# An experts' layer between two attention stages: norm, logits, routing and row sends as steps of the first layer's blocks, the fallback in pieces behind the last block

## The chip, the cores and the metric

The kernel runs on one core of a Trainium2 chip. The metric is device time in microseconds (us) of one execution. The engines are PE (TensorE: matrix products, transposes), DVE (VectorE), ACT (ScalarE), POOL (GpSimd) and SP (SyncE, which here only issues DMAs).

## What is computed

The input x has 16 sequences of 256 tokens with 128 features, all f32: 4096 tokens. Four residual steps follow each other.

```python
x = x + linear_attention(norm(x))     # 32 heads of 4, two decays, a norm at its end
x = x + experts(norm(x))              # 8 experts, two per token, at most 1280 tokens each
x = x + decay_attention(norm(x))
x = x + local_attention_and_ffn(norm(x))   # 2 layers
```

The second step is the one that the change is about:

```python
probs = softmax(x_flat @ Wr.T)
scores, experts = top_k(probs, 2);  scores = scores / scores.sum(-1)
cap = 1280                                    # int(1.25 * 4096 * 2 / 8)
y_fb = ffn(x_flat, fw1, fb1, fw2, fb2)        # the fallback, for every token
y = 0; fallback = False
for e in range(8):
    match = (experts == e)
    elig = match.any(-1) & ~fallback          # tokens, in order
    pos = cumsum(elig) - 1
    kept, overflow = elig & (pos < cap), elig & (pos >= cap)
    y[kept] += ffn(x_flat[kept], W1[e], b1[e], W2[e], b2[e]) * weight
    y = where(overflow, y_fb, y); fallback = fallback | overflow
```

`ffn` is a gelu between two products (128 to 512 and back). A token that overflows an expert takes the fallback's output and takes part in no later expert.

## The kernel before

**Tiles and blocks.** The tokens form 32 tiles of 128 rows (NT), and 8 blocks of four tiles (NB). All of x stays in SBUF. "Normal" tiles hold tokens in the partitions; turned ones (`hT`) hold features in them.

**First stage, lines 263 to 563, by hand.** A class `Linear` (line 364) has the steps of one block as methods: `measure_x`, `rows_x`, `turn` (norm and transposes of the input), `rotate`, `raised`, `feature` (queries and keys), `gates`, `clip`, `spread_beta`, `value`, `weigh`, `scan` (446, a DVE scan of 128x512 for each of 2 decays m and of 5 columns cc), `product` (451, POOL, scan by query), `den`, `share`, `query`, `add` (477, PE sums of the products into the bank `y`), `gather`, `project` (486, into the bank `z`), `measure_z`, `rows_z` (the norm at the end) and `close` (502, three POOL operations of 128x512 that add the block's result to x). A class `Spread` (335) keeps mean and variance for one iteration; one square root on ACT serves all of them. The loop at 511 runs t = -2 to 9 under `tc.manual_schedule()`: the order of instructions in the program is the order on each engine. In iteration t, block t is scanned, t+1 is projected, t+2 is measured and turned, t-1 is finished, and t-2 is closed.

**Second stage, lines 565 to 819, by a planner.** Outside the hand-written order a planner orders the instructions of each engine by their costs and due times. SP issues the loads of the last stage's weights (570 to 587). Then come the statistics of all 32 tiles (helper, lines 245 and 246), normalisation on DVE (655), transposes (656), the logits (660, 661), the routing of all 32 tiles at once (679 to 744), and the 64 sends (748 to 753): each is an indirect DMA issued by POOL that scatters the 128 rows of a tile from `hn` to the slots of their expert in `xs`, in DRAM. The routing counts, for each of the 8 experts in turn, the tokens ahead (two PE products with constant tables and a DVE scan over tiles, 718 to 733), since an overflow changes what later experts see. For each block, lines 773 to 792 add the experts' bias by weights (`w9`, turned by PE, times `b2row`, line 783) and the fallback's output by its weight (788). The fallback and the experts share `ffn` (663): four pairs of `ph` products with gelu on ACT (669) into `hid`, then `py` products. The experts (795 to 817) read `xs` in 8 x 3 chunks of 512, 512 and 256 rows (`xe`, SP, line 800), turn them (805), copy them (807, DVE), run `ffn`, and store `ye` into `ys` (811, 812).

**Last stage, from line 822.** Rows are fetched from `ys` by 64 gathers (1035, POOL), then decay attention, local attention and the last ffn follow. The change leaves it alone.

In the listing, `mm` (line 128) is the helper that records most products, so these groups have the line L128 in the profile.

Of the kernel before, what the change touches and what calls it, by code (L numbers as in the profile page):

```python
# [18 lines left out]
P = 128  # L19
BATCH = 16  # L20
SEQ = 256
D = 128
# [31 lines left out]
def _layout():  # L54
    at, n = {}, 0
    for name, width in (
        ("ident", P), ("sel", 4 * P), ("blk", NH0), ("rep4", P), ("cos", SEQ), ("sin", SEQ),
        ("behind", P), ("rep8", P), ("xpos", 4 * 2 * DH), ("desc", NE),
    ):
        at[name] = (n, width)  # L60
        n += width
# [3 lines left out]
def _tables():  # L65
# [39 lines left out]
    put("desc", np.tile(np.arange(NE, 0, -1, dtype=f4), (P, 1)))  # L105
    return c
# [16 lines left out]
def tile_kernel(ctx: ExitStack, tc: tile.TileContext, i: dict, out: bass.AP, last: int = 4):  # L123
# [124 lines left out]
    def rstd(mv, n=NT):  # L248
        r = small.tile([P, n], F32, tag="rstd", name="rstd")
        act.activation(r, mv[:, :, 1], AF.Sqrt, bias=eps)  # L250
        dve.reciprocal(r, r)
        return r

    def normalize(eng, o, a, mv, r, n):
        eng.tensor_scalar(o, a, mv[:, n, 0:1], r[:, n : n + 1], ALU.subtract, ALU.mult)

    def transposed(ps, name, n=P):
        t = ps.tile([P, BW], F32, tag="tr", name="wtr")
        pe.transpose(t[:, :n], nat[name], ident[:n, :n])
        return t[:, :n]  # L260


    with ExitStack() as c:
# [6 lines left out]
        po = c.enter_context(tc.tile_pool(name="a_po", bufs=1, space=PSUM))  # L270
# [64 lines left out]
        class Spread:  # L335


            def __init__(self):
                self.mv = wk.tile([P, 8, 2], F32, tag="mv", name="mv", bufs=3)
                self.lo, self.hi = 8, 0  # L340
# [5 lines left out]
            def sqrt(self):  # L346
                if self.lo > self.hi:
                    return
                self.rs = wk.tile([P, 8], F32, tag="rs", name="rs", bufs=3)
                self.nm = wk.tile([P, 8], F32, tag="nm", name="nm", bufs=3)  # L350
# [13 lines left out]
        class Linear:  # L364
# [6 lines left out]
            def measure_x(self, sp):  # L371
                for j in range(4):
                    sp.take(4 + j, x[:, 4 * self.b + j, :])

            def rows_x(self, sp):
                self.h = wtile("h", 2)
                for j in range(4):
                    sp.row(self.h[:, js(j)], x[:, 4 * self.b + j, :], 4 + j)
# [107 lines left out]
            def project(self):  # L486
                self.z = po.tile([P, BW], F32, tag="po", name="po")
# [5 lines left out]
            def measure_z(self, sp):  # L493
                for j in range(4):
                    sp.take(j, self.z[:, js(j)])

            def rows_z(self, sp):
                self.o = wk.tile([P, 4, D], F32, tag="o", name="o")
                for j in range(4):
                    sp.row(self.o[:, j, :], self.z[:, js(j)], j)  # L500
# [7 lines left out]

        blocks = [Linear(b) for b in range(NB)]
        with tc.manual_schedule():  # L510
            for t in range(-2, NB + 2):
# [4 lines left out]
                sp = Spread()  # L516
                do(0, "scan", 0, HD0)
                do(0, "scan", 1, HD0)
                do(0, "product", 0, HD0)
                do(0, "product", 1, HD0)  # L520
                do(2, "measure_x", sp)
                do(1, "rotate", "k")
                do(-1, "add", 1, HD0 - 1)
                do(-1, "gather")
                do(1, "rotate", "q")
                do(0, "den")
                do(-1, "project")
                do(1, "gates")
                do(0, "share")
# [770 lines left out]
```

## Time and profile before

| | us |
|---|---|
| median of 3 runs | 1548.76 (1547.97 to 1551.07) |
| the profiled execution | 1548.69 |
| its span, from first to last instruction | 1546.9 |
| PE busy | 1240.1 (80%) |
| DVE busy | 979.6 (63%) |
| POOL busy | 831.6 (54%) |
| ACT busy | 770.6 (50%) |
| granted clock of PE, mean | 0.900 |
| end of the last product of block 7 (first stage) | 253.3 |
| end of block 7's `close` | 266.0 |
| first and last send | 327.8 and 408.4 |
| first matmul of an expert's chunk (transposes, line 805) | 453.8 |
| start of the last stage (about) | 616.8 |

The busy times are shares of the whole span and so say little about a stage. The profile's page also has the span in 40 slices of 38.7 us, with a digit for each engine (9: 90% or more busy) and for PE's clock. A group of instructions is named by its line, engine, operation and tiles (out<-in), with its count, its busy time and the mean of one in ns. The chain of waits goes back from the last instruction to what released each; "issue" in it is time in which an engine waited for nothing that the profile shows, "remote" in a wait is a semaphore whose setter the profile doesn't name. SPq is SP's DMA queue, PEld is the load of PE's weights.

### The profile page before, as it was taken

What the parts mean: (1) busy time and instruction counts of PE and PEld (TensorE: products, weight loads), DVE (VectorE), ACT (ScalarE), POOL (GpSimd) and SP (SyncE); (2) the same over time, 40 slices, a digit from 0 to 9 for tenths busy, and PEclk for the clock granted to TensorE, in tenths of its full rate; (3) what the DMA queues carried; (4) which work ended last, traced back from release to release, by engine and by line L of the source; (5) the groups of instructions that cost most, each with busy time, mean ns of one, the idle gap of its engine ahead of it and who ended that gap; (6) DMA issues with size and microseconds to landing.
All of it is one profiled execution on the core that took longest, in us unless ns stands there. A gap on an engine that the chain in (4) does not pass through costs nothing.

```text
span 1546.9 us, 26264 instructions
## 1 busy us (share of the span) xinstructions
PE 1240.1 (80%) x9793; PEld 817.4 (53%) x9793; DVE 979.6 (63%) x2316; ACT 770.6 (50%) x1478; POOL 831.6 (54%) x822
## 2 busy tenths in 40 slices
PE   5788785870299999265688788899999999999996
PEld 2334433650267777132355465666666666666673
DVE  4999985540021111357887787888778887878862
ACT  4443521310033333134556657776777767677653
POOL 1577775047400000668877765776676767767521
PEclk9989896775599999567898899999999999999998
DMA  7300000201102221100111111111111111111110
GB/s 225 136 1 1 1 1 32 65 26 51 56 11 68 69 68 34 36 24 17 39 29 32 29 24 23 26 24 33 26 26 31 26 31 33 38 33 26 38 34 16
DMA packets 67450, 59.41 MB, mean 38 GB/s; under 512 B 16905, under 2 KB 53754, under 8 KB 67322
## 3 DMA queue, kind: packets, MB, share of 16 engines
q1 hardware_dynamic: 62402, 48.12, 11.7%
q0 software_dynamic: 4096, 8.40, 1.7%
q8 instruction: 78, 1.28, 0.3%
q10 hardware_dynamic: 824, 1.20, 0.2%
q14 instruction: 50, 0.41, 0.1%
HBM read 21.78 MB, written 16.78 MB: 25 GB/s over the span
## 4 chain that ended last, share of the span: by engine, by line
PE 41%; DVE 24%; issue 9%; ACT 7%; DMA 1%; POOL 0%; POOLq 0%; another core or an unknown queue 0%; ACTq 0%; DVEq 0%
PE pm L128 9%; PE py L128 7%; PE pq L128 7%; PE ph L128 7%; DVE rot L878 3%; PE S L128 3%; DVE ss L879 3%; ACT hn L1158 2%; DVE x L1044 2%; DVE bnst L245 2%; PE pm L996 2%; PE pm L974 2%; PE pm L932 1%; DVE o L991 1%; DVE ex L963 1%
## 5 line engine op out<-in xcount | busy, mean ns | idle before, releaser
L881 POOL TENSOR_TENSOR t<-t,tabs 128x512 f32<-128x512 f32 x128 | 164.4, 1285 | 141.0 <-ACT t L876 140.6
L669 ACT ACTIVATE hid<-ph,b1c 128x512 f32<-128x512 f32 (+1 forms) x128 | 79.8, 633 | 184.9 <-PE ph L128 119.6
L883 POOL TENSOR_TENSOR rot<-rot,t 128x512 f32<-128x512 f32 x128 | 163.1, 1274 | 10.0
L921 POOL TENSOR_TENSOR rot<-rot,rn 128x512 f32<-128x512 f32 x128 | 130.7, 1042 | 40.4 <-DVE rn L900 40.4
L878 DVE TENSOR_TENSOR rot<-pq,tabs 128x512 f32<-128x512 f32 x128 | 87.7, 685 | 79.1 <-ACT t L876 77.7
L128 PE MATMUL pq<-wqkv,hT 128*128 128x512 f32 x256 | 134.4, 651 | 0.8 <-DVE rot L878 0.8
L998 ACT COPY oT<-pm 128x512 f32<-128x512 f32 x64 | 37.1, 580 | 188.6 <-PE pm L996 183.3
L841 POOL MEMSET mhalf<- 128x1 f32 x1 | 0.1, 104 | 206.4 <-ACT hid L669 206.4
L453 POOL TENSOR_TENSOR s<-s,q 128x512 f32<-128x512 f32 x64 | 83.7, 1317 | 38.2 <-DVE s L449 20.2
L750 POOL DMA_INDIRECT xs<-hn,r_into x64 | 62.4, 975 | 76.9 <-DVE r_into L740 57.7
L962 DVE TENSOR_REDUCE ng<-S 128x4 f32<-128x512 f32 x128 | 87.4, 683 | 23.0 <-PE S L128 21.2
L811 DVE COPY ye<-py 128x512 f32<-128x512 f32 (+1 forms) x24 | 14.5, 603 | 135.5 <-PE py L128 135.5
L963 DVE TENSOR_TENSOR ex<-S,ng 128x512 f32<-128x512 f32 x128 | 88.5, 692 | 4.6
L874 ACT ACTIVATE sq<-pq 128x512 f32<-128x512 f32 x128 | 77.6, 606 | 27.0 <-PE pq L128 22.0
L879 DVE TENSOR_REDUCE ss<-sq 128x8 f32<-128x512 f32 x128 | 86.5, 676 | 0.0
L128 PEld LDWEIGHTS pm<-vs,pT 128*64 128x64 f32 x1024 | 64.5, 137 | 38.8 <-issue 11.1
L128 PEld LDWEIGHTS py<-w,hid 128*128 128x128 f32 x640 | 77.6, 192 | 12.9 <-issue 8.6
L996 PE MATMUL pm<-cf,o 128*128 128x128 f32 x256 | 43.3, 294 | 49.6 <-DVE o L991 49.6
L128 PE MATMUL ph<-xT,w 128*128 128x512 f32 (+1 forms) x192 | 75.3, 528 | 7.7 <-DVE xT L807 7.7
L128 PE MATMUL py<-w,hid 128*128 128x128 f32 x640 | 80.0, 277 | 0.0
L967 ACT ACTIVATE ex<-ex 128x512 f32<-128x512 f32 x128 | 76.4, 662 | 3.1 <-DVE ex L963 2.8
L932 PE MATMUL pm<-cf,rot 128*128 128x128 f32 x512 | 70.2, 276 | 9.3 <-POOL rot L921 6.5
(293 smaller groups left out, 3345.4 us busy)
## 6 DMA issues: line engine op xcount, KB each, us to landing
vs<-v SPq DMA_DIRECT2D x128, 130.0 KB
xs<-zeros SPq DMA_DIRECT2D x10, 512.0 KB
w<-in_L_ffn_W_dram SPq DMA_DIRECT2D x16, 256.0 KB
xe<-xs SPq DMA_DIRECT2D x16, 256.0 KB
ys<-ye SPq DMA_DIRECT2D x16, 256.0 KB
x<-in_L_attn_x_dram SPq DMA_DIRECT2D x8, 256.0 KB
out_dram<-x SPq DMA_DIRECT2D x8, 256.0 KB
up<-u SPq DMA_DIRECT2D x32, 56.0 KB
```

The lines of the kernel that those rows point to most:

```text
L128: pe.matmul(o, lhsT, rhs, start=start, stop=stop)
L453: pool.tensor_tensor(s, s, self.f["q"] if cc == HD0 else self.q[m], ALU.mult)
L669: act.activation(hid[:, ci, :width], t[:, :width], AF.Gelu, bias=b1c[:, bias0 + ci : bias0 + ci + 1])
L874: act.activation(sq, ps, AF.Square)
L878: dve.tensor_tensor(heads(rot[:, k, :]), heads(ps), wide(tabs[l][:, 2 * k, a, :]), ALU.mult)
L879: dve.tensor_reduce(ss[:, j, k, :], heads(sq), AX.X, ALU.add)
L881: pool.tensor_tensor(heads(t2), heads(t2), wide(tabs[l][:, 2 * k + 1, a, :]), ALU.mult)
L883: pool.tensor_tensor(halves(rot[:, k, :]), halves(rot[:, k, :]), halves(t2)[:, :, ::-1, :], ALU.add)
L921: pool.tensor_tensor(ro, ro, rn, ALU.mult)
L932: pe.transpose(ps[:, hp * P : (hp + 1) * P], self.rot[:, k, hp * P : (hp + 1) * P], ident)
L962: dve.tensor_reduce(ng[:, q, :], self.S[q], AX.X, ALU.max, negate=True)
L963: dve.tensor_tensor(ex[:, q], self.S[q], ng[:, q, :].unsqueeze(2).to_broadcast([P, 4, P]), ALU.add)
```

## The change

1. **Norm, logits.** After `close`, a block's x is measured (`measure_n`), and one iteration later normalised on ACT (`rows_n`, formerly DVE), turned (`turn_n`) and given its logits. All statistics share the iteration's `Spread` (12 columns, formerly 8). `close` moves from block t-2, ahead of the products, to block t-1, behind the first half of them. `add` is grouped: the four of m=0 at cc=0, the four of m=1 at the start of the next iteration. The bank of `z` is now that of `y`, and the bank that came free serves the routing.
2. **Routing by groups of tiles.** `Route(lo, hi).steps()` is a generator that handles a range of tiles, and hands back at each `yield`; `tick()` runs it to the next. Tiles 0 to 7 begin at t=4, 8 to 15 at t=6, 16 to 23 behind the loop, then 24 to 27 and 28 to 31. The first group can't overflow (1024 tokens, 1280 slots) and counts all experts at once; the others go expert by expert, and start from the counts of the group before.
3. **Sends.** `send(3)` behind `query` and `send(2)` at the end of an iteration put sends on POOL, each behind a memset of a 128x1 tile, `spare`; 20 of the 64 are issued inside the loop (t=4 to 7). Those of the tail follow as 6, 2, and then whatever is routed.
4. **Tail.** The loop ends at t=7. The rest of blocks 6 and 7 is written out by hand, with pieces of the fallback between (`fill`). There are 64 pieces: 32 of a `ph` product and gelu, 32 of eight `py` products. The fallback's result overwrites the turned tile in `hT`, and waits there.
5. **Second stage.** It keeps the shares, `w9`, and the experts; the bias and the fallback's weighted result are added by `residual(e)`, one block behind each expert.

The diff, cut to its core:

```diff
@@ class Linear
             def project(self):
-                self.z = po.tile([P, BW], F32, tag="po", name="po")
+                self.z = py.tile([P, BW], F32, tag="py", name="po")
...
+            def measure_n(self, sp):
+                for j in range(4):
+                    sp.take(8 + j, x[:, 4 * self.b + j, :])
+            def rows_n(self, sp):
+                for j in range(4):
+                    sp.row(hn[:, 4 * self.b + j, :], x[:, 4 * self.b + j, :], 8 + j)
+            def turn_n(self):
+                pt = bank("nt")
+                for j in range(4):
+                    pe.transpose(pt[:, js(j)], hn[:, 4 * self.b + j, :], ident)
+                act.copy(cols_n(self.b), pt)
+            def logits(self):
+                pl = bank("pl")
+                for j in range(4):
+                    mm(pl[:, j * NE : (j + 1) * NE], hT[:, 4 * self.b + j, :], wr)
+                dve.tensor_copy(lg[:, 4 * self.b : 4 * self.b + 4, :].rearrange("p n e -> p (n e)"), pl[:, : 4 * NE])
+        class Route:
+            def steps(self):
...
+                if hi * P <= CAP and lo == 0:
+                    m = match.rearrange("p e n -> p (e n)")
...
+                    mm(pos, con("behind"), m)
+                    mm(tot, ones, m)
+                    yield
...
+                else:
...
+                    for e in range(NE):
...
+                        dve.tensor_tensor(el, match[:, e, :], ok, ALU.mult)
+                        mm(tot, ones, el)
+                        mm(pos, con("behind"), el)
+                        yield
+                        before = Route.counts[:, e, -1:] if lo else 0.0
+                        dve.tensor_tensor_scan(run[:, e, :], ones[:, 0:n], tot, before, ALU.mult, ALU.add)
+                        dve.tensor_tensor(r, run[:, e, :], pos, ALU.add)
+                        dve.scalar_tensor_tensor(over, r, float(CAP), el, ALU.is_gt, ALU.mult)
+                        dve.tensor_tensor(ok, ok, over, ALU.subtract)
...
+                for j in range(lo, hi):
+                    rows.extend([(j, 0), (j, 1)])
+        def send(most):
+            for _ in range(min(most, len(rows))):
+                j, k = rows.pop(0)
+                pool.memset(spare, 0.0)
+                sent.append(pool.indirect_dma_start(
+                    out=xs, out_offset=bass.IndirectOffsetOnAxis(ap=into[k][:, j : j + 1], axis=0),
+                    in_=hn[:, j, :], in_offset=None, bounds_check=SLOTS - 1, oob_is_err=False,
+                ))
+        def fallback():
...
+            for b in range(NB + 1):
+                hid[b] = []
+                for ci in range(NIC):
+                    if b < NB:
+                        t = bank("fh")
+                        mm(t, fw1[:, ci * P : (ci + 1) * P], cols_n(b))
+                        h = wtile(f"kv{ci}")
+                        at_ = NE * NIC + ci
+                        act.activation(h, t, AF.Gelu, bias=b1c[:, at_ : at_ + 1])
+                        hid[b].append(h)
+                        yield
+                    if b:
+                        outward(b - 1, ci)
+                        yield
@@ the loop
-            for t in range(-2, NB + 2):
+            for t in range(-2, NB):
...
-                sp = Spread()
+                sp, later = later, Spread()
+                if t == 4:
+                    work.append(Route(0, 8).steps())
+                elif t == 6:
+                    work.append(Route(8, 16).steps())
                 do(0, "scan", 0, HD0)
                 do(0, "scan", 1, HD0)
+                tick()
                 do(0, "product", 0, HD0)
                 do(0, "product", 1, HD0)
                 do(2, "measure_x", sp)
+                tick()
                 do(1, "rotate", "k")
-                do(-1, "add", 1, HD0 - 1)
+                tick()
+                for cc in range(HD0):
+                    do(-1, "add", 1, cc)
                 do(-1, "gather")
...
-                do(-2, "close")
+                tick()
+                send(3)
                 sp.scales()
...
                 do(2, "rows_x", sp)
+                do(-2, "rows_n", sp)
                 for cc in range(HD0):
                     do(0, "product", 0, cc)
...
+                do(-1, "close")
                 do(1, "feature", "k")
...
                 for cc in range(HD0):
                     do(0, "scan", 1, cc)
+                    tick()
                     do(1, "weigh", cc)
-                    do(0, "add", 0, cc)
+                    if cc == 0:
+                        for c2 in range(HD0):
+                            do(0, "add", 0, c2)
...
                     if cc == 1:
                         do(1, "feature", "q")
                         do(2, "turn")
+                        do(-2, "turn_n")
+                        if t == 1:
+                            prepare()
+                    if cc == 2:
+                        do(-2, "logits")
                     do(0, "product", 1, cc)
-                    if cc:
-                        do(0, "add", 1, cc - 1)
+                do(-1, "measure_n", later)
                 do(1, "spread_beta", 1)
+                send(2)
@@ the tail
+            work.append(Route(16, 24).steps())
+            tick(2)
...
+            last_b.project()
+            both(2)
+            send(6)
+            last_b.measure_z(sp)
...
+            last_b.close()
+            send(2)
...
+            last_b.logits()
+            work.append(Route(24, 28).steps())
+            work.append(Route(28, 32).steps())
+            while work:
+                both(1)
+                send(NT)
+            for _ in fb:
+                pass
@@ the second stage
-        for b in range(NB):
+        def residual(b):
...
-            ffn(hT[:, 4 * b : 4 * b + 4, :].rearrange("p n t -> p (n t)"), BW, fw1, NE * NIC, fw2, add_fallback)
+            for n in range(4 * b, 4 * b + 4):
+                dve.scalar_tensor_tensor(x[:, n, :], hT[:, n, :], w9[:, n, NE : NE + 1], x[:, n, :], ALU.mult, ALU.add)
 
         for e in range(NE):
...
                 ffn(xT[:, :width], width, w1[:, e, :], e * NIC, w2[:, e, :, :], keep)
+            residual(e)
```

`both(n)` is n times a `tick()` and a piece of the fallback. The statistics, normalisation, logits, routing, sends and fallback of the second stage (lines 644 to 661, 679 to 753 and 773 to 792) are removed. `prepare` makes `wr` and `b1c` (formerly lines 597 to 603).

## The prediction

> **What bounds the kernel now.** I read four views: the 40 slices, then the windows (busy time by stage), then the chain and the waits where PE stands, then the timeline around its two ends. The slices first:
>
> ```profile
> PE   5788785870299999265688788899999999999996
> DVE  4999985540021111357887787888778887878862
> POOL 1577775047400000668877765776676767767521
> PEclk9989896775599999567898899999999999999998
> ```
>
> One slice is 38.7 us. The 2nd to the 7th are the first layer's loop, with DVE highest; the 8th to the 16th are the experts' stage, and in it the 10th holds a PE of 0 and the 11th of 2, while POOL stands at 7 and 4. From 616.8 us the last stage runs, 930.1 us, which the change doesn't touch. By stage (window, its length, busy PE, PEld, DVE, ACT, POOL, clock, DMA):
>
> ```profile
> 127.55:155.49 27.94, 23.15 (x128) 11.30 (x128) 25.82 (x43) 11.59 (x26) 20.23 (x19) 0.94 0.00 1
> 360.00:380.00 20.00, 0.00 (x0) 0.00 (x0) 0.00 (x0) 0.00 (x0) 15.43 (x16) 0.50 0.15 53
> 414.00:616.80 202.80, 194.98 (x1143) 148.63 (x1144) 35.60 (x72) 70.34 (x116) 1.01 (x3) 0.98 0.17 49
> ```
>
> The first is one iteration of the loop: DVE bounds it, with 2.1 us to spare. The third is the end of the fallback and the experts: PE bounds it, 96% busy. In the second only POOL works. What stands there, by the chain (start, us, what), by the waits between 336 and 432 (engine, line, what it waited for: us in all, times, longest) and by the costliest groups:
>
> ```profile
> 340.54 2.88 PE py L128 x24
> ...
> 352.37 61.72 issue
> 414.08 2.07 PE bw L128 x8
> ```
> ```profile
> ACT hid L669 <- remote: 63.9, 1, 63.9
> ...
> PE bw L128 <- issue: 61.7, 1, 61.7
> DVE x L788 <- remote: 54.6, 1, 54.6
> ```
> ```profile
> L750 POOL DMA_INDIRECT xs<-hn,r_into x64 | 62.4, 975 | 76.9 <-DVE r_into L740 57.7
> ```
>
> The 64 sends run from 327.8 to 409.4, one each 1.27 us (0.97 and 0.30 of issue). PE goes on for 16 us of them, some 12 sends; then it gives one matmul per 0.7 us, and from 352.4 nothing until 414.1, 4.7 us after the last send. The chain calls it "issue": no semaphore of another engine ended it. That the dense row of sends does it is my reading; its onset after 12 sends I use below. So between the last product of block 7 (ends 253.3) and the first expert (453.8) lie 200 us, of which 62 are PE standing, 61 are norm and routing with every engine half idle, and the rest is mostly fallback.
>
> **Part 1, the loop.** Each of its iterations gets statistics of x after `close` (4 x 0.40 = 1.6 us of DVE), a row step (4 x 0.4 ACT), 4 transposes (0.60 PE), a copy (0.58 ACT), logits (1.0 PE) and their copy (0.19 DVE). ACT has 16 us free in 27.94, and hides its part; PE has 4.8. What is not hidden is the order: turn, copy, turn_n, copy, logits, copy stand in front of `scan(1,3)` on DVE, 0.6+0.58+0.6+0.58+1.0+0.19 = 3.55, less some 1.4 that the copy and the product before it already covered: +2.1. The statistics at the end add 1.6 to DVE, of which about 0.6 lies beside PE's own chain: +1.0. So t=2..5: 4 x 3.1 = 12.4; t=6 without the statistics' wait: 2.1; `prepare` at t=1: 1.3. At t=7, `close` (3 x 1.27 on POOL) now stands ahead of the products of the second half, and no next block's work covers it, +4.1; and the two sends that t=6 issues at its end stand ahead of the first products (2 x 1.45, less 0.8 in which POOL waits for the scans), +2.1: 6.2. In t=5 and t=6 I leave that to the next part. The grouped adds cost nothing more: 8 such matmuls ran in 1.06 us, as long as 2 alone:
>
> ```profile
> 142.06 1.06 PE L128 MATMUL y<-s,cfa 128*32 128x512 f32 x8
> 143.41 1.04 PE L128 MATMUL y<-s,cfa 128*32 128x512 f32 x2 [0.28 <-POOL s L453]
> ```
>
> Routing on DVE: the operations of 128x32 in the old routing took 0.18 to 0.22 us, those of 128x256 0.42; for 8 tiles (64 columns) I take 0.21. Route(0,8) has 26: 5.5. Route(8,16) has 65: 13.6, less 2.6 that fall into DVE's gaps: 11. Bounds for the two: all hidden in gaps (2.1 us x 4 = 8.4 less), or each operation also waiting for PE's answer (8 answers at 0.9, as the old one did: +7). Sum for the loop: 12.4+2.1+1.3+6.2+5.5+11 = +38.5; block 7's last product ends at 292 (bounds 280 and 305).
>
> **Part 2, the sends in the loop.** 20 of them, 5 in each of t=4..7, each with a memset of 0.1 us: 1.45 us of POOL. POOL has 20.23 + 7.25 = 27.5 of an iteration that is now about 31: hidden, at nothing; if it isn't, up to 20 x 1.45 = 29 us. Behind a send on POOL stand the products, for which PE's adds wait. An indirect transfer beside a busy DVE is shown in the last stage: its gathers (line 1035) took 997 to 1092 ns, middle 1026, against 972 in the idle burst, so +5%.
>
> The Trainium skill ("SBUF — State Buffer", section "SBUF: two separate sides") speaks against this: a DMA issued by GpSimd needs the port that VectorE's fast modes hold, and one of some 620 ns took 3100 beside such work. By that, 20 sends would cost an estimated 20 x 2.5 = 50 us, and the forecast would come to 1565 instead. This case's gathers at 1026 ns beside a DVE 80% busy speak for the row.
>
> **Part 3, the tail.** POOL from 292: 8 sends 11.6, `close` 3.8, 2 sends 2.9: 310. Block 7's norm to logits ends near 320. Then Route(24,28) and Route(28,32), each 8 experts at about 1.9 us (2.16 with matmuls between, 1.86 alone in the old one) and 6 around them: 21, so 341 and 362. The sends follow in rows of 20, 8 and 8; the last 8 begin at 362 and end at 373.6, land by 376 (a send landed 2.3 us after its issue).
>
> The fallback: 32 pieces of 2 ph (1.02) and 32 of 8 py (0.83): 58 us of PE. 38 pieces lie beside norm and routing, 26 behind: 26 x 0.95 = 25, so 387. The weights of the last stage (SP: `fa` to `maskb`, lines 573 to 587), formerly issued from 266.06 to 278.8, wait for `spare`'s last memset (372) and take 12.7 us of SP; the experts' first rows stand behind them: 388, with their landing. That cover is the fallback; without it these are 12 us late.
>
> Does PE stand again? Rows of 8 are below the 12 at which it began; the row of 20 is above: 8 sends x 1.45 and 4.7 behind them, 16 to 17 us in which Route(24,28), which needs PE, stands too. I take it, as the nearest row shows it; without it, 0. Experts start at 388 + 17 = 405.
>
> **Part 4, the experts.** 163 us (453.8 to 616.8) stay. The residual moves into them, once for each of 8: 4 transposes 0.45 to 0.60 and 4 pieces of bias 1.1 on a PE that has no room: 1.6, so 12.8 (bounds 8 and 17). DVE's 0.69 + 4 x 0.28 each has room (35.6 of 202.8). Small steps at the start (outof, e2, shares): 2, on DVE under the first ph.
>
> **Sum:** 405 + 163 + 12.8 + 2 = 583, against 616.8: -34. The profiled execution had 1548.69 us, 1546.9 of span and 1.79 around it, 0.07 from the median of 1548.76; so 1515.
>
> **Rivals.**
> *No standing:* pauses of other POOL work between sends (memsets) keep PE free: 388 instead of 405, **1498**. For it: 12 sends did PE nothing. Against: a memset is only 0.1 us. 20%.
> *No room in the loop:* the sends delay products, and each costs its full 1.45: +29, **1544**. For it: POOL's 20.2 are spread along the chain and not in one gap. Against: 3 of 5 stand where POOL waits for DVE. 13%.
> *Slower:* PE's signals come late in every row of sends, from the first on; then nothing overlaps a send. Place: the tail, where sends, routing and fallback became one chain. Loop 292 + 4 x 3 = 304; 8 sends, close and 2 to 323; block 7's logits 333; 20 sends and 4.7: 367; Route 388; 8 sends 404; Route 425; 8 sends 441; the fallback that had no cover, 11: 452; experts 178: 630, +13.5, **1562**. It decides once the experts begin after 616.8 - 178 = 439, that is when the tail grows by 34 us beyond my 405. For it: DVE stood at L783 until 346.88 for a product that PE had finished at 340.5, some 10 sends in. Against: PE's own matmuls went on at full rate until then. 14%.
> *It doesn't do what it says:* the routing in steps is fully serial with the scans (each step waits for PE), so that the loop gives 25 us more than I count while the rest holds: **1540**. 5%.
>
> **Numbers.** The forecast 1515 has 48% with its own range 1500 to 1532 (loop 280 to 305, experts -5 to +4). Differences of 0.2%, 3 us, are the least that measurement can tell. Faster: 0.48+0.20+0.13+0.04 = 0.85, less 0.05 for the upper ends of the terms together: 0.80; same 0.04; slower 0.16. The range goes from 1486 (no standing, low loop) to 1556 (no room, with the upper bounds).
>
> **What would show it.** Right: the iterations t=2..5 at about 31 us, t=6 and 7 near 38; no sends longer than 1.1 us; PE idle only in the row of 20; experts from about 405 at 22 us each. Wrong: a PE gap at the rows of 8 or in the loop; products waiting behind sends for over 5 us an iteration; the first expert waiting for its rows from SP.

## The result, and the profile after

The changed kernel is slower by 0.4%: 1557.22 us (1551.89 to 1561.04, 13 runs) beside 1550.37 (13 runs) for the kernel before in the same comparison, a ratio of 1.0042 (95% interval 1.0028 to 1.0056). The forecast was 1515, with 1486 to 1556 as range. The profiled execution has a span of 1558.4.

The slices of the changed kernel (38.96 us each):

```profile
PE   5778676776959999355678788899999999999996
DVE  4898787624122222356887787787787878878762
POOL 1576574763200000577977756666767676766621
PEclk9998786777879999666898899999999999999999
```

The hole with a PE of 0 is gone; behind the loop PE has 7, 6 and 9, and then a 5 in the twelfth slice. But DVE's digits at the start stay at 6 or more up to the eighth slice, before only up to the sixth, and the last `ye`, the end of the experts, ends at 627.1, 9.5 us later than before (617.6). By stage (us, busy PE, PEld, DVE, ACT, POOL, clock, DMA): iterations t=4 and t=6, the stretch ahead of the experts, and the experts:

```profile
153.11:195.13 42.02, 27.72 (x141) 15.77 (x141) 33.00 (x78) 13.71 (x29) 24.31 (x26) 0.78 0.02 6
227.95:277.57 49.62, 33.83 (x168) 22.93 (x169) 36.92 (x109) 11.69 (x24) 25.50 (x29) 0.70 0.02 7
433.80:448.60 14.80, 0.02 (x1) 0.02 (x1) 4.43 (x22) 0.03 (x1) 0.10 (x1) 0.57 0.85 264
448.60:630.00 181.40, 173.19 (x1008) 129.46 (x1008) 40.88 (x88) 63.19 (x105) 0.10 (x1) 0.99 0.19 54
```

An iteration that lasted 27.94 us lasts 42.0 with the routing of tiles 0 to 7, and 49.6 with that of tiles 8 to 15. DVE is busy 6.6 and 10.3 us more than in t=3 and t=5, close to the 5.5 and 11 that were counted; the rest of the growth, 3.5 and 6.5 us, is idle time of DVE. PE is busy 2.1 and 8.7 us more, at a granted clock of 0.78 and 0.70 beside 0.83 and 0.87 in t=3 and t=5. Ahead of the experts PE does nothing for 14.8 us while the DMA moves 264 GB/s.

The sends are as long as before, in the loop too:

```profile
L643 POOL DMA_INDIRECT xs<-hn,into x64 | 62.7, 979 | 57.4 <-issue 35.0
```

Where the 45 us between forecast (span 1513) and measurement lie:

| from | to | forecast | measured | difference |
|---|---|---|---|---|
| start | block 7's last product | 292 | 306.5 | +14.5 |
| that | routing's end | 87 (with 17 of standing) | 100.3 | +13.3 |
| that | fallback's end on PE | 25 | 23.7 | -1.3 |
| that | first transposes of an expert | 1 | 18.1 | +17.1 |
| that | last `ye` | 178 | 178.5 | +0.5 |
| that | end | 930.1 | 931.3 | +1.2 |

Three terms are off: the loop, the way to the routing's end, and the way to the experts. The longest waits between 300 and 470 us name the last two (engine, line, what it waited for: us in all, times, longest):

```profile
DVE lg L537 <- remote: 22.5, 1, 22.5
...
PE et L960 <- DMA xe<-xs: 14.8, 1, 14.8
```

The first is a late signal: an engine that waits for PE's result goes on only long after PE has finished it. This is PE's timeline and then DVE's and ACT's around it (start, us, operation, idle before and its releaser):

```profile
345.24 1.88 PE L129 MATMUL pl<-wr,hT 128*128 128x8 f32 x8 [5.11 <-ACT hT L531]
346.97 2.05 PE L129 MATMUL fh<-hT,fw 128*128 128x512 f32 x2
348.81 1.91 PE L129 MATMUL fo<-fw,kv 128*128 128x128 f32 x8
360.34 2.07 PE L129 MATMUL fh<-hT,fw 128*128 128x512 f32 x2 [9.62 <-DVE lg L537]
```
```profile
360.10 0.19 DVE L537 COPY lg<-pl 128x32 f32<-128x32 f32 x1 [22.50 <-remote]
...
344.60 0.58 ACT L531 COPY hT<-nt 128x512 f32<-128x512 f32 x1 [4.60 <-remote]
```

PE has finished the logits `pl` at 347.1; DVE, which waits for nothing else, begins their copy at 360.1, 2.9 us after the last send of the row (357.2). DVE's own signal reaches PE at once (360.29 to 360.34). So it is what PE sends out that is late, by 13 us. (The profile models the ends of matmuls; whether the product itself or only its signal was late can't be told from it.) The same row had delayed a signal to ACT before: PE ended the transposes `nt` at 338.4, when seven sends of the row were out; ACT was free from 340.0, but began their copy at 344.60, and the logits waited for it.

The second is SP. Its queue in the trace:

```profile
430.70 0.38 SPq L832 DMA_DIRECT2D wqkv<-in_L_ffn_wqkv_dram  x1
431.12 0.47 SPq L835 DMA_DIRECT2D fa<-in_L_ffn_w_dram  x1
...
442.77 0.43 SPq L849 DMA_DIRECT2D maskb<-in_masks_dram  x1
443.30 6.79 SPq L955 DMA_DIRECT2D xe<-xs  x5
```

The first load is issued right behind PE's last product of the fallback (430.5), and all 17, 12.6 us of issue, stand ahead of the experts' rows `xe`.

### The profile page after: what moved, and what is told of

Read it like the earlier page. It is cut to its first block, busy times and chain, and to the rows that moved or that the text cites. A ratio compares the mean times of both kernels' runs of the same rounds, so it can differ in the third digit from the quotient of the medians.

```text
span 1558.4 us, 26730 instructions
## 1 busy us (share of the span) xinstructions
PE 1267.4 (81%) x9893; PEld 844.4 (54%) x9893; DVE 1005.3 (65%) x2494; ACT 791.3 (51%) x1522; POOL 839.9 (54%) x888
## 4 chain that ended last, share of the span: by engine, by line
PE 26%; DVE 21%; ACT 7%; issue 3%; DMA 1%; POOL 0%; POOLq 0%; another core or an unknown queue 0%; ACTq 0%; DVEq 0%
PE pm L129 9%; PE pq L129 7%; DVE rot L1034 3%; PE S L129 3%; DVE ss L1035 3%; ACT hn L1314 2%; DVE x L1200 2%; PE pm L1152 2%; DVE bnst L246 2%; PE pm L1130 2%; PE pm L1088 1%; DVE o L1147 1%; DVE ex L1119 1%; DVE ng L1118 1%; DVE qT L1091 1%
## 5 line engine op out<-in xcount | busy, mean ns | idle before, releaser
L129 PE MATMUL pq<-wqkv,hT 128*128 128x512 f32 x256 | 138.3, 667 | 0.8 <-DVE rot L1034 0.8
L966 DVE COPY ye<-py 128x512 f32<-128x512 f32 (+1 forms) x24 | 14.5, 603 | 133.5 <-PE py L129 133.5
L904 ACT ACTIVATE hid<-ph,b1c 128x512 f32<-128x512 f32 (+1 forms) x96 | 57.3, 616 | 78.9 <-PE ph L129 78.2
L643 POOL DMA_INDIRECT xs<-hn,into x64 | 62.7, 979 | 57.4 <-issue 35.0
L129 PEld LDWEIGHTS py<-w,hid 128*128 128x128 f32 x640 | 77.7, 192 | 14.5 <-issue 9.6
L1130 PEld LDWEIGHTS pm<-cf,ex 128*128 128x128 f32 x512 | 60.1, 141 | 32.2 <-issue 22.8
```

Of the source, the lines that this page charges most:

```text
L129: pe.matmul(o, lhsT, rhs, start=start, stop=stop)
L1130: pe.transpose(ps[:, hp * P : (hp + 1) * P], self.ex[:, q, hp, :], ident)
```

## The experiments

Each run has the kernel before beside it on the same chip. The chips differ: on some the kernel before takes 1550 to 1553 us, on others 1512 to 1513. Runs of different chips are compared by their ratio to the kernel before, or stage by stage. Letters e and f are only names.

**The kernel before and the changed kernel again** (unchanged copies).

> The kernel before, once more, for its trace on this chip. The chip of the runs e1 to e4 gave it 1512.57 us where the first profile had 1548.7, and no late signal in their row of sends. If the late signals of PE are a property of the chip or of the execution: where the time is near 1512, PE goes on through the 64 sends (no wait over 5 us between 340 and 400), the fallback ends near 390, the experts' first rows come right behind the last send (about 414), and the last stage is unchanged at 929. Rival (the chip is faster throughout): every stage is 2 to 3% shorter, and PE still stands some 60 us.

> The changed kernel, once more, beside the kernel before on the same chip. If there are no late signals on this chip: the logits reach DVE near 338, the routing ends near 378, the fallback near 401, PE then waits some 18 us for SP's weights, and the experts begin near 420; 1531, which is 1.2% above a kernel before of 1512. If there are late signals: as in the first trace, the logits near 360, and 0.4% above the kernel before.

Measured: 1512.74 for the kernel before (7 runs; the traced copy 1512.46), 1529.33 for the changed one, ratio 1.0114 (1.0083 to 1.0146). In the kernel before the loop ends at 254.3 and the last stage takes 927, close to the 253.3 and 929 of the first profile: the chip isn't faster throughout. What is missing is the standing. Its windows (as above) and the wait that replaces it:

```profile
360.00:380.00 20.00, 18.90 (x111) 13.31 (x109) 3.63 (x10) 7.46 (x12) 15.23 (x16) 1.00 0.15 52
380.00:412.00 32.00, 0.00 (x0) 0.00 (x0) 0.00 (x0) 0.00 (x0) 23.32 (x24) 0.53 0.15 51
```
```profile
PE et L805 <- DMA xe<-xs: 35.8, 1, 35.8
```

Here PE works through the sends, has all of the fallback but its last 26 products done at 379, and then waits only for the last sends: experts from 414.7 instead of 450.4. (Both are the first transpose of an expert's chunk, which stands ahead of those 26 products in PE's order; the 453.8 given ahead of the prediction is the transposes behind them.) The changed kernel there has its logits at 342.7, routing's end at 382.7, and the experts at 424.4. So the experts begin 36 us earlier in the kernel before on a chip without late signals, 24 in the changed kernel, and the change loses more. What follows: the late signals are there on some chips only, and they are not what makes the change slower than before; they hurt both. (Each chip was seen on one occasion only, so whether it is the chip or the occasion isn't told apart.)

**SP's order** (e1):

```diff
-    nc.sync.dma_start(out=wqkv, ...)      # and the 16 that follow, ahead of the experts
+    def load_last(): nc.sync.dma_start(out=wqkv, ...)   # the same 17
...
             residual(e)
+            if e == 0:
+                load_last()
+                make_tabs()
```

> The 16 loads of the last stage's weights (and the tables made from them) stand behind the first expert's three loads on SP instead of ahead of them. Theory (SP's queue holds the experts back: the weights wait for tiles that the fallback uses, to 430.7, and then take 12.6 us of issue ahead of the first rows): PE's idle 14.8 us before the first expert shrink to about 3, so some 12 us less, near 1545. Rival (the rows themselves are late, since the last sends only land at about 419, or the first experts then lack rows behind the loads): the gap returns before the second expert, and the time stays within 4 us of 1557.

Measured: 1517.12, ratio 1.0031 (1.0015 to 1.0047), on a chip where the kernel before takes 1512.57. Against the changed kernel's 1.0114 on a chip of the same kind that is 0.83% or 12.6 us. SP and PE in its trace:

```profile
402.39 1.74 SPq L958 DMA_DIRECT2D xe<-xs  x3
404.24 0.40 SPq L840 DMA_DIRECT2D wqkv<-in_L_ffn_wqkv_dram  x1
```
```profile
405.83 1.09 PE L963 MATMUL et<-cf,xe 128*128 128x128 f32 x8 [0.31 <-DVE lamc L875]
```

The experts begin 3.6 us after the fallback's end (402.2) instead of 18. This is what the theory expected. The expected absolute time didn't fit, as it took the first chip's. (The tables made from these weights moved with them.)

**The row of sends, on a chip without late signals** (e2 to e4).

```diff
+            del rows[:20]                                  # e2, e3
+            for _ in range(20):                            # e3
+                pool.tensor_tensor(zeros[:, 0:BW], zeros[:, 0:BW], zeros[:, BW : 2 * BW], ALU.add)
             while work:
                 both(1)
-                send(NT)
+                send(NT, True)                             # e4: such an addition behind each send
```

> Leaves out the 20 sends that stand in a row behind block 7's close, so part of the experts' rows is missing. Theory (PE's signals come late while sends follow each other densely): DVE's wait for the logits (22.5 us, to 360.1) goes, the logits reach DVE at about 341, and routing, fallback and experts come about 19 us earlier: near 1538. Rival (the wait is the chain of norm, table loads, copies and fallback pieces itself): less than 5 us.

> As the run that leaves out 20 sends, but with a 128x512 addition on POOL (1.27 us, as long as a send with its issue) in place of each. If it is the sends' transfers that delay PE's signals: as that run, within 3 us, near 1538, with the logits at DVE by about 341. If a busy POOL, by whatever it holds, delays them: as the changed kernel, the logits at about 360 and 1557.

> All sends stay; each send from the row of 20 on is followed by a 128x512 addition on POOL, so one send each 2.6 us instead of 1.27. If the density delays PE's signals: the logits reach DVE near 341 to 345 and no wait for PE is over 3 us; the last sends come a little later (20 sends now take 52 us, to about 381), and the time falls by 10 to 19 us. If it is the number of sends in the last tens of us, whatever their spacing: a stand again from about the 12th send, with the same length or twice it.

Measured: 1532.37, 1535.5 and 1535.59; the logits at DVE at 337.1, 336.6 and 336.3 in all three. But e1, on the same chip, with the whole row, had them at 338.4. So nothing was there to remove, and these three tell nothing of the cause. (e2 and e3 leave out part of the experts' rows.)

**The same on a chip with late signals** (f1 the changed kernel, f3 and f4 as e3 and e4; all three on one chip, one run each).

> The changed kernel as the control of this call. On a chip where the kernel before takes about 1550: the logits of block 7 reach DVE about 13 us after PE's last product of them, 22 us in all, as in the first trace, and 1557. On one where it takes 1512: no such wait, and 1530.

> Leaves out the 20 sends in the row behind block 7's close and puts a 128x512 addition on POOL (1.27 us) in place of each. To be read beside the control of this call, where that has the late signals. If the transfers delay PE's signals: the wait of the logits is under 5 us, and the time 17 to 21 us below the control. If a busy POOL does: wait and time as in the control. Where the control has no such wait it tells nothing.

> All sends, each from the row of 20 on followed by such an addition: one send each 2.6 us instead of 1.27. To be read beside the control of this call, where that has the late signals. If the density of the sends delays PE's signals: no signal over 3 us late, and the logits at DVE near 341. If their number does: a stand from about the 8th to the 12th send, lasting until the row ends at about 380.

Measured: 1556.63, 1552.12 and 1545.23, with 1553.2 for the kernel before. The waits of f1 between 340 and 362 us, then of f3 (333 to 362) and of f4 (340 to 362):

```profile
DVE run L614 <- remote: 10.5, 1, 10.5
...
ACT kv L669 <- remote: 7.5, 1, 7.5
```
```profile
DVE run L614 <- PE rt L129: 5.1, 6, 1.4
```
```profile
DVE run L614 <- PE rt L129: 6.5, 8, 1.2
```

In f1 the logits were through at 342.7, ahead of the onset, and the routing's counts stood instead; the expectation had the place wrong, not the kind. DVE had its answer 9.9 us and ACT 6.5 us after PE's end. With additions in place of the sends no signal was late in that stretch (ACT's longer waits there, up to 7.5 us, ended within 0.1 us of the end of PE's product): it isn't POOL's being busy. With all sends, one each 2.5 us, none was late either, over 20 sends: it isn't their number. From the loop's end to the routing's end passed 99.7 us in f1, 86.3 in f3, 80.9 in f4 (loop's end at 304.0, 307.0 and 302.5). f3 still has its rows of 8 sends at full density behind the logits, and from there to the routing's end it takes 47.4 us, f4 40.5. In that row of 8 one answer reached DVE 2.2 us after PE's end (376.1 to 378.32), so rows of 8 do it too, if less; what the rest of the 7 us is isn't resolved. So the density of the sends makes PE's signals late on this chip. f3's time lay only 4.5 us below f1's, where 17 to 21 were expected. f4's fell by 11.4, though its routing ended 20.2 us earlier: its fallback ended at 405.4, but its last memset of `spare` at 415.77, and SP's first load came at 415.79. So the loads wait for both, the memset and the fallback.

**The loop without sends, and without routing** (e5, e6; the chip of c_after).

```diff
-                send(3)
...
-                send(2)
...
-                if t == 4:                                  # e6
-                    work.append(Route(0, 8).steps())
-                elif t == 6:
-                    work.append(Route(8, 16).steps())
...
+            work.append(Route(0, 8).steps())                # e6, behind the loop
+            work.append(Route(8, 16).steps())
             work.append(Route(16, 24).steps())
```

> The 20 sends of the loop move behind it, into the rows of the tail; the routing stays in the loop. Prediction's theory (sends in the loop hide in POOL's gaps): the loop's last product ends within 2 us of where it ends in the changed kernel (302 to 306). Rival (they delay products): 5 to 15 us earlier. In either case the tail has 20 sends more in its rows, about 26 us of POOL, of which most lies beside routing.

> Neither sends nor routing in the loop: all three first groups are routed behind it. What is left in the loop is norm, transposes and logits. By the prediction that costs 22 us (279 minus the loop's old end, 253.3, and what t=4 and t=6 have for routing, 16.5, taken off): last product near 275. Rival (routing in the loop costs what the iterations t=4 and t=6 show, 10.1 and 16.8, since PE's counting products stand ahead of the loop's own): near 306 - 27 = 279 or less, 276 to 279 with the sends' share. Between these the iterations decide: t=4 and t=6 should be as long as t=3, 31 to 32.

**The counting products one step later** (e9; a chip with late signals).

```diff
+                    yield
                     mm(pos, con("behind"), m)
...
                         dve.tensor_tensor(el, match[:, e, :], ok, ALU.mult)
+                        if hi <= 16:
+                            yield
                         mm(tot, ones, el)
```

> The changed kernel, with the routing's counting products of the first two groups issued one step later, so that DVE has made their input before PE comes to them. If PE's standing ahead of the loop's own products is what makes t=4 and t=6 longer than the DVE time that they were costed at: t=4 falls from 42.0 to about 39, and t=6 from 50 by 6 and more (its routing spreads to t=7, which may gain some of it back); the loop ends 5 to 9 us earlier. If it is DVE time alone: the loop ends within 2 us of 303 to 306, and only t=6 and t=7 share otherwise.

Length of each iteration of the loop in us, from one scan of the keys to the next (t=7: to block 7's last product), and the loop's end. The edits of e1 to e4, f1, f3 and f4 leave the loop alone, so with the two traces of the changed kernel it was measured nine times:

| | t=1 | t=2 | t=3 | t=4 | t=5 | t=6 | t=7 | end |
|---|---|---|---|---|---|---|---|---|
| before | 27.6 | 28.1 | 27.9 | 27.9 | 28.7 | 28.0 | 24.5 | 253.3 |
| forecast | 28.9 | 31.1 | 31.1 | 36.6 | 31.1 | 41.1 | 30.7 | 292 |
| changed | 29.5 | 30.8 | 31.9 | 42.0 | 32.8 | 49.6 | 29.0 | 306.5 |
| changed, other chip (c_after) | 29.3 | 30.8 | 31.9 | 42.0 | 31.3 | 50.6 | 28.4 | 304.9 |
| the same loop, lowest and highest of nine | 28.1 to 29.5 | 30.8 | 30.8 to 32.0 | 40.6 to 42.0 | 31.3 to 33.0 | 47.5 to 50.6 | 28.4 to 29.2 | 299.9 to 307.0 |
| no sends (e5) | 29.5 | 30.9 | 30.8 | 39.9 | 30.9 | 49.0 | 28.7 | 300.9 |
| no routing either (e6) | 28.1 | 30.8 | 30.8 | 30.8 | 30.9 | 29.5 | 28.3 | 272.4 |
| products later (e9) | 28.1 | 30.8 | 30.8 | 37.0 | 32.6 | 35.4 | 34.7 | 290.9 |

e5 took 1526.39 and e6 1517.96 (before: 1512.74), one run each. e5: its loop ends 4 us earlier than c_after's, but within the spread of the nine; t=4 to t=7, which hold the sends, take 148.5 us together, beside 149.5 to 153.5 in the nine. So the sends cost the loop 1 to 5 us of their 29, which is hardly clear of the spread. e6: norm, transposes and logits alone bring it to 272.4 (forecast 275). Routing therefore costs 28.5 us in the loop, not 16.5. e9 has the same operations as the changed kernel, and its t=4 to t=7 take 139.7 us, 10 to 14 less than in the nine: 5.0 in t=4 and 8.4 in t=6 and t=7 together, beside the first trace. That is more than was expected. DVE's busy time in t=6 and t=7 is 57.9 us there, beside 56.5; only its idle time went. The wait at which the edit aims, in the changed kernel and then in e9, each from t=6's start to the loop's end:

```profile
PE rt L129 <- DVE els L609: 11.9, 7, 2.6
```
```profile
PE rt L129 <- DVE els L610: 10.5, 3, 4.2
```

Seven times PE came to a counting product before DVE had its input, and what stood behind it on PE, the loop's own sums and projections, stood too. In e9 this happened three times, but for almost as long in all. What also changed is PE's own time: 48.0 us busy in t=6 and t=7 beside 54.9 for as many instructions, at a granted clock of 0.77 beside 0.70. So the order and pace of the routing's steps is shown to cost 10 to 14 us; how much of it is standing behind a product, how much the slower PE, and how much the spreading of the second group over t=7, isn't shown. e9 took 1544.09 (before: 1553.25), one run.

**Versions put together** (e7: e6 with SP's order of e1; e8: groups of 8, 12 and 12 tiles and ten sends behind block 7's `close`; e10: the logits behind the scans).

```diff
-            work.append(Route(8, 16).steps())               # e8
-            work.append(Route(16, 24).steps())
+            work.append(Route(8, 20).steps())
...
-            work.append(Route(24, 28).steps())
-            work.append(Route(28, 32).steps())
+            work.append(Route(20, 32).steps())
...
-                    if cc == 2:                              # e10
-                        do(-2, "logits")
                     do(0, "product", 1, cc)
+                do(-2, "logits")
                 do(-1, "measure_n", later)
```

> The routing of the first three groups and the 20 sends behind the loop (as in the run without routes in the loop), and the last stage's weights behind the first expert's rows on SP. If the two costs are independent: the experts begin some 14 us earlier than in the run without routes in the loop (408), near 394, and 1503 on a chip where the kernel before has 1512. If the sends, whose last stands at 387, hold the rows: the experts begin after 400, 1510.

> As the run before it, but the routing in three groups of 8, 12 and 12 tiles instead of five of 8, 8, 8, 4 and 4, and ten sends instead of two behind block 7's close. A group that goes expert by expert costs 20 to 22 us whatever its size (the answers of PE set it, not the 0.16 to 0.27 us of an operation): two of them instead of four, so the routing ends some 25 us earlier, near 352; the fallback on PE then sets the start of the experts, near 378. Together near 1487. Rival (the cost goes with the tiles, or POOL's 64 sends of 82 us from 277 on set it): routing or sends still end after 375, and the gain over the run before is under 8 us.

> As the run with three groups, but the logits and their copy on DVE stand behind the last scan of an iteration, not ahead of it. The prediction put 2.1 us an iteration (t=2 to 7) on the chain of turns, copies and logits ahead of that scan. If that was right: 2 us less in each of t=2 to t=6, the loop ends 8 to 11 us earlier than in that run, and the time is lower by as much. If DVE is the bound anyway, or the chain then delays the statistics behind it: under 3 us.

Measured, all on a chip with late signals (before: 1553.25): 1546.33, ratio 0.9956 (0.9940 to 0.9972); 1531.14, 0.9865 (0.9841 to 0.9888); 1518.03, 0.9788 (0.9762 to 0.9814). e7's experts begin at 430.7, not at the 394 expected for a chip without late signals: the 64 sends now all stand in rows behind the loop and the signals are late (five waits of the routing for them, 32.1 us in all). e8's routing ends 50 us earlier than e7's (360.2 beside 410.3), twice what was expected, with two such waits, 21.9 us; its experts begin 13 us earlier. That a group pays for its eight answers of PE, and more where they are late, fits this, but the groups and the ten sends weren't tried apart. e10's iterations t=2 to t=5 take 29.1 to 29.2 us (e8: 30.8 to 30.9), its loop ends 10.3 us earlier, at 259.4, as expected. From its experts' start at 405.3, beside 450.4, 45 us are gained, and 15 given back in the experts' stage (181.9 beside 167.2). e10 beats both kernels on such a chip. On one without late signals it wasn't run.

**The first group back in the loop** (e11: e10 with tiles 0 to 7 routed at t=4, products a step later, and their 16 sends in the loop).

> As the run with three groups and the logits behind the scans, but the first group (8 tiles, no overflow) is routed at t=4 in the loop with its counting products a step later, and its 16 sends go out in the loop. If routing costs its DVE time there (6 us) and the sends next to nothing, the loop ends 6 to 9 us later, but the tail has 16 sends (20 us of POOL) and 6 steps less: 3 to 12 us below that run where PE's signals come late in rows of sends (below 0.979 of the kernel before, about 0.972), and 0 to 5 us below elsewhere. If the sends in the loop delay products by their full length: 16 x 1.3 = 21 more in the loop, and slower than that run.

Measured: 1535.75, ratio 0.9882 (0.9865 to 0.9898), where about 0.972 was expected: slower than e10 by 0.94% of the kernel before. The loop ends at 276.8: t=4 takes 34.8 us (+5.7, as expected for the routing), but t=5, t=6 and t=7, with sends alone, 30.8, 30.5 and 30.9 beside 29.2, 26.7 and 25.8. That is 10.5 us in iterations that got nothing but sends, in a loop that is tighter than the one of e5. That the sends push products there is the likely reading; no run has this loop with the routing and without the sends, and t=7 alone varies by 2 us (27.9 in e13, which has the loop of e10). And the tail isn't shorter: 140 us from the loop's end to the fallback's end, with 142 in e10; PE's signals are late in its rows as well.

**Pauses between the sends of e10** (e12: a 128x256 addition behind each; e13: 128x128).

> The run with three groups and the logits behind the scans (0.979 of the kernel before on a chip with late signals), with a 128x256 addition on POOL (about 0.7 us) behind each send: one send each 2.0 us. If that is sparse enough: no signal of PE over 3 us late, the routing ends near 325 and the fallback near 365; the 64 sends then take 128 us and end at about 385 to 395, and the experts begin right behind, 8 to 15 us earlier than that run's 405: 0.970 to 0.974. If the delay sets in at this density too: waits of 5 to 15 us as before, the experts near 410, 0.98. On a chip without late signals the pauses only cost: experts near 395 by the sends, 0.99.

> The same with a 128x128 addition (about 0.4 us): one send each 1.7 us. If the limit lies between 1.3 and 1.7 us: no late signals, the sends end near 375, the experts near 382: 0.963 to 0.967, better than with the longer pause. If it lies above: late signals as without pauses, experts at 400 or later, 0.977 and more. On a chip without late signals: experts near 380, 0.98.

Measured, on a chip without late signals: 1512.30, ratio 0.9994 (0.9984 to 1.0004), and 1500.39, 0.9908 (0.9887 to 0.9929). Expected for such a chip were 0.99 and 0.98. One send each 1.95 and 1.68 us; the experts wait for the last of them (first transposes at 399.2 and 389.7, 5 us behind its start). These runs don't bound the density from which signals come late, as none was late here: between one each 1.27 and one each 2.5 us stays open. They show that the rest of e10 holds on such a chip: even with pauses e13 beats the kernel before.

## Why the prediction was wrong, point by point

1. **What bounds the kernel.** Right for the chip of the first profile. PE's standing is the work of the dense sends (f3, f4), but it is not a property of the kernel alone: the first profile and two of five later chips (e7 to e10; f1 to e11) had it, the other three did not (the chip of e12 and e13 counted by its 1512.64 us for the kernel before).
2. **Norm and logits in the loop, 22 us.** Right within 4 us: 18 (272.4 in e6, with 254.3 in the kernel before on the same chip). The 2.1 us for the chain ahead of `scan(1,3)` was 1.7 (e10).
3. **Routing in the loop.** This step failed: "Route(0,8) has 26: 5.5. Route(8,16) has 65: 13.6, less 2.6 that fall into DVE's gaps: 11." The operations were sized right: DVE was busy 6.6 and 10.3 us more. But t=4 and t=6 grew by 10.1 and 16.8, and routing cost the loop 28.5 us (e5 beside e6), not 16.5. What was left out is that the counting products are also entries in PE's queue, and that their place and pace there costs the loop more than DVE's time: 10 to 14 us of it went in e9 with the same operations. The upper bound had the answers to DVE (8 at 0.9) in it, but not what stands behind the product on PE. (The signs at the end of the prediction gave 38 us for t=6 and t=7; its own terms give 41.1 and 30.7.)
4. **Sends in the loop, nothing.** Nearly right: 1 to 5 us (e5), perhaps up to 10 in a tighter loop (e11). The rule of the Trainium skill ("SBUF — State Buffer", section "SBUF: two separate sides"), by which they would have cost an estimated 50, doesn't show: the 64 sends of the changed kernel took 966 to 1212 ns on POOL, middle 972, those in the loop among them. No row here tells which of DVE's operations beside them ran in a fast mode.
5. **Standing in the row of 20, 17 us.** The kind was right, the size short, and the onset wrong. From the loop's end to the routing's end passed 100.3 us, with 77.8 on the chip without late signals: 22.5 more, 15.8 of them up to the logits and 6.7 behind, where the rows of 8 stand. The forecast had 87, with 70 without the standing. "Rows of 8 are below the 12 at which it began" went by PE's own stop; PE's signals were late earlier than that, in the first trace after seven sends, and a row of 8 delayed an answer too (f3, by 2.2).
6. **SP.** This step failed: "wait for `spare`'s last memset (372)" and "That cover is the fallback". The memset was right (f4), but the first load waits for the end of the fallback as well, and so isn't beside it. The text gave 12 us for the case without cover; it came out as 17 (12.6 of issue, and landing).
7. **Experts.** Right: 178.5 with 178 forecast. (The forecast counted the kernel before from 453.8; from 450.4, as below, the last 3 us of its fallback stand in the 167.2.)
8. **Rivals.** "Slower" named 1562 and experts from 452, near the measured 1557 and 448.6, but that is luck: signals were prompt for the first sends of a row, part of the loss lay in the loop and at SP, and without any late signal the change is slower still (1.0114). "No standing" did occur, on other chips, and there the kernel before had none either; the forecast had treated it as a matter of the changed kernel alone. "Fully serial routing" was nearest to what happened in the loop, which ended 14.5 us late where it gave 25.

Where the gain went: from the loop's end to the first expert the changed kernel takes 142.1 us, the kernel before 197.1, so 55 were won. The loop gave back 53 of them (306.5 beside 253.3), the experts' stage 11 (178.5 beside 167.2), the last stage 2: 11.5 us slower in the two profiles (6.9 by the medians). e10 takes the routing out of the loop, makes three groups of it, moves the logits behind the scans and SP's loads behind the first expert's rows, and is 2.1% faster than the kernel before where signals are late.

## What to carry to other kernels

When work is moved into a loop whose order is written by hand, price it on each queue that it enters, not only on the engine that computes it: a product whose input is not ready stops everything behind it, and one step more between the two cost nothing here (e9). When a stage is moved earlier, look at what else was released by the end of the stage before it (here SP's loads), and now is released later. And a gap that a profile calls "issue" may belong to the chip: run the kernel before on another one before pricing its removal.

## What the runs showed of the hardware

On three of six occasions PE's signals to other engines came late while POOL issued indirect transfers one each 1.27 us: after some 7 to 12 of them, by 4.6 and 13 us in the first trace, 6.5 and 9.9 in f1. In the first trace the last came through 2.9 us after the row's last send; in f1 both came before the row's end. A signal from DVE to PE in the same stretch was prompt (0.05 us). At one send each 2.5 us there was none late (f4), nor with additions of about equal length in place of the transfers (f3), one run each. In the kernel before on the first chip PE itself stopped (61.7 us), and the busier of the two DMA queues of the kind "instruction" (q8 in the page) moved no packet from 315 to 415 us; on a chip without late signals it moved two in that stretch, near 347 and 366. Whether fetches and signals share a path with the transfers wasn't tried, and why chips differ stays open. The same program took 1512 us on some chips and 1550 on others, and nearly all of the difference (35.7 of 36.2 us between the two profiles) lay ahead of the first expert.
